# Two small DMAs on another queue, reordered scores, and roots on another engine, in a fused attention and expert kernel

## The chip, the cores and the metric

The kernel runs on one core of one Trainium2 chip. The core has five engines with instruction queues of their own: TensorE (matrix products and transposes, PE in the profile, its weight loads PEld), VectorE (DVE), ScalarE (ACT), GpSimd (POOL) and SyncE (SP, which here only issues DMAs). Each engine works through its queue in order; engines wait for each other through semaphores. ScalarE and POOL can issue DMAs too, each on a queue of its own. The metric is the device time of one execution in microseconds, lower is better.

## The reference

Sixty-four batches of 256 tokens with 256 features go through two layers. Each layer is a graph attention with a residual, then a feed-forward part with a residual; each of the four parts begins with a normalization of every row.

```python
def _layernorm(x, axis=-1, eps=1e-5):
    m = jnp.mean(x, axis=axis, keepdims=True)
    v = jnp.var(x, axis=axis, keepdims=True)
    return (x - m) / jnp.sqrt(v + eps)

# --- layer 0 (adj_ffn) ---
x = x + _L0_gnn_ref(_layernorm(x, axis=-1), adj, L0_gnn_W, L0_gnn_a)
x = x + _L0_ffn_ref(_layernorm(x, axis=-1), L0_ffn_weight, L0_ffn_bias)
# --- layer 1 (adj_ffn) ---
x = x + _L1_gnn_ref(_layernorm(x, axis=-1), adj, L1_gnn_W, L1_gnn_a)
x = x + _L1_ffn_ref(_layernorm(x, axis=-1), L1_ffn_router_w, ...)
```

The first attention has four heads of 64, leaky scores e_src[i] + e_dst[j] masked by the adjacency, a softmax over j and an ELU; the second has one head and a ReLU. The last part is a mixture of eight experts (256 to 256, GELU, 256 to 256), of which each token uses two, chosen by a router and weighted by a softmax over the two.

## The kernel before

**Batches.** One generator, `batch_layers`, holds the work of one batch: the first norm and projection (L569 to L575), the scores and the attention with four heads (L584 to L609), the linear layer (L611 to L628), the second attention (L629 to L653), the last norm (L655 to L662), then the row `xe` for the experts and the router's logits (L664 to L706). A batch is spread over several steps of an outer loop (L1194), and a new batch begins every third step (`TICKS = 3`), so several batches are in flight at different stages.

**Order.** The order of instructions on each engine is written out by hand. A generator yields a rank, and within a step the pieces of all active jobs are issued by rising rank (L1222 to L1229). A positive rank ends the job's part of this step; a negative one (`yield -36`) continues in the same step at rank 36. All queues follow this order, so an instruction with a higher rank stands behind the others of its step on its engine.

**The terms.** For the first attention the terms of a batch that lie along the columns are turned on VectorE (`ut`, L505), written to DRAM by a 4 KB DMA (L579) and read back spread over all 128 partitions by a second DMA of 512 KB (L514), which has to wait until the first has landed. Both are issued by SyncE, among the loads of later batches and, in the first 80 us, the loads and repacking of the eight experts' weights (`pack_expert`, L278). VectorE then computes the scores in two halves of four instructions (L530): the first at rank 10, the second at rank 70. Between them, at rank 40, come the reciprocals of the second attention of an earlier batch (L551), and ScalarE needs those for `rel` (L644).

**The norms.** For a norm, VectorE's batch statistics (L375, L376) or squares on ScalarE with accumulation (L402) give the variance; POOL computes (variance + eps)^-0.5 with two small instructions (L383 and L384, or L412 and L415). Two norms of different batches share one pair of these instructions, as their values are put in one tile: the first waits for the second, or for the end of the step (L1230 to L1233).

**Experts.** The rows of the first 61 batches are sent to DRAM regions, one for each expert, by indirect DMAs of POOL (L1011). They come back as pairs of 128 rows (`expert_pair`): loads on SyncE, a transpose on VectorE (L117), the first product (L903), two Gelus on ScalarE (L909), the second product (L918), the bias (L928), the row weight (L896). POOL then adds each pair's rows to the output by two indirect DMAs (L939). Adds of one pair wait until those of the pair before have landed, since they may meet in a row. Copies on ScalarE need no function table; Exp and Gelu lie in different tables, and a switch is an instruction of its own (ACT_TABLE_LOAD). The last three batches are computed for all experts without routing (`dense_expert`, L957). From step `DRAIN_AT` (three steps for each of B - 5 batches) pairs are started in every step; the stage after the last batch has begun is called the drain here.

**The transposes.** The linear layer's result x2 is transposed on TensorE in four pieces (L421) and copied by ScalarE (L427), at rank 36. The first product of a pair stands at rank 30, so it comes first. The projection of the second attention (L472, one step later) needs the copy.

Of the kernel before, what the change touches and what calls it, by code (L numbers as in the profile page):

```python
# [27 lines left out]
def kernel(  # L28
# [17 lines left out]
    nc = tc.nc  # L46
    B, N, D = x.shape
# [4 lines left out]
    NT = N // P  # L52
    EPS = 1e-5
# [6 lines left out]
    CHUNKS = (4,) * 12 + (2,) * 5 + (1,) * 3  # L60
# [9 lines left out]
    TICKS = 3  # L70
# [4 lines left out]
    small = ctx.enter_context(tc.tile_pool(name="small", bufs=4))  # L75
# [49 lines left out]
        return ap.rearrange("p (a k) -> p k a", k=KT)  # L125

    AHEAD, BLOCKS_AHEAD = 3, 2


    ident = const.tile([P, P], F32, tag="ident", name="ident")  # L130
# [228 lines left out]


    half_done = []

    def norm_stats(src):

        stats = small.tile([P, NT, 6], F32, tag="stats", name="stats")
        if half_done:
            mv, rstd = half_done[0]
            at = NT
        else:
            mv = small.tile([P, 2 * NT, 2], F32, tag="mv", name="mv", bufs=4)  # L370
            rstd = small.tile([P, 2 * NT], F32, tag="rstd", name="rstd", bufs=5)
            half_done.append((mv, rstd))
            at = 0
        for t in range(NT):
            nc.vector.bn_stats(stats[:, t, :], src[:, t, :])  # L375
            nc.vector.bn_aggr(mv[:, at + t, :], stats[:, t, :])  # L376
        if at:
            finish_norms(2 * NT)
        return mv[:, at : at + NT, :], rstd[:, at : at + NT]

    def finish_norms(n):
        mv, rstd = half_done.pop()
        nc.gpsimd.tensor_scalar_add(rstd[:, :n], mv[:, :n, 1], EPS)  # L383
        nc.gpsimd.tensor_tensor(rstd[:, :n], rstd[:, :n], mhalf[:, :n], ALU.pow)  # L384

    half_squared = []
# [3 lines left out]

    def norm_squares(src, sums):
        if half_squared:
            sq, rstd = half_squared[0]
            at = NT
        else:
            sq = small.tile([P, 2 * NT], F32, tag="sq", name="sq", bufs=4)
            rstd = small.tile([P, 2 * NT], F32, tag="rstd", name="rstd", bufs=5)
            half_squared.append((sq, rstd))
            at = 0
        for t in range(NT):  # L400
            off = work.tile([P, D], F32, tag="off", name="off", bufs=1)
            nc.scalar.activation(  # L402
                off, src[:, t, :], AF.Square, bias=sums[:, t : t + 1], scale=-float(D),
                accum_out=sq[:, at + t : at + t + 1],
            )
        if at:
            finish_squares(2 * NT)
        return rstd[:, at : at + NT]

    def finish_squares(n):  # L410
        sq, rstd = half_squared.pop()
        nc.gpsimd.tensor_scalar(  # L412
            rstd[:, :n], sq[:, :n], 1.0 / D**3, EPS, op0=ALU.mult, op1=ALU.add
        )
        nc.gpsimd.tensor_tensor(rstd[:, :n], rstd[:, :n], mhalf[:, :n], ALU.pow)  # L415
# [44 lines left out]
    for i in range(2):  # L460
        t = keep.tile([P, NT, D + 1], F32, tag=f"q1_{i}", name=f"q1_{i}")
# [39 lines left out]
    def send_terms(q, b):  # L501


        ut = small.tile([P, S], F32, tag="ut", name="ut", bufs=1)
        nc.vector.transpose(  # L505
            ut.rearrange("p (t h w) -> p t h w", t=NT, h=H), q[:, :, :, HD - 1 : HD + 3]
        )
        ud = tc.dram_tile([S, S], F32, name=f"terms_{b}")
        ud = ud.rearrange("c r -> (c r)").rearrange("(c p) -> c p", p=P)
        return ut, ud  # L510

    def spread_terms(ud, z):

        nc.sync.dma_start(  # L514
            out=z[:, NT - 1].rearrange("p t h i -> p (t h i)"),
            in_=rows_to_all(ud, S * S),
        )

    def scores(q, z, hs, spread):

        for h in hs:
            terms = z[:, NT - 1, :, h, :]
            if not spread:
                terms = bank("pd", [NT, P])
                for t in range(NT):
                    nc.tensor.transpose(
                        terms[:, t, :], q[:, t, h, HD + 1 : HD + 2].to_broadcast([P, P]), ident
                    )
            for j in range(NT):
                nc.vector.scalar_tensor_tensor(  # L530
                    z[:, j, :, h, :], terms, q[:, j, h, HD + 2 : HD + 3],
                    masks[0][:, j, :].rearrange("p (t i) -> p t i", t=NT),
                    op0=ALU.max, op1=ALU.mult,
                )
# [19 lines left out]
    def batch_layers(b, c0, xng, lg):  # L554

        def first_norm():
            x0 = xin.pop(b)
            if b + AHEAD < B:
                xin[b + AHEAD] = load_batch(b + AHEAD)
            return x0, norm_stats(x0)[1]  # L560

        if b:
            x0, rstd = first_norm()
# [6 lines left out]
        if not b:  # L570
            x0, rstd = first_norm()
# [4 lines left out]
        if b:  # L576
            ut, ud = send_terms(q, b)
            yield -31
            nc.sync.dma_start(  # L579
                out=ud.rearrange("c (g r) -> g c r", g=G),  # L580
                in_=ut[2 : P : S // (NT * H), :],
            )
            yield -52
        z = work.tile([P, NT, NT, H, P], F32, tag="z4", name="z4", bufs=2)  # L584
        if b:
            spread_terms(ud, z)
        yield 99
        yield 10
        scores(q, z, range(0, 2), b > 0)
        yield -70  # L590
        scores(q, z, range(2, 4), b > 0)
# [19 lines left out]
        _, rstd = norm_stats(x1)  # L611
# [24 lines left out]
        z = scores1(ex, me)  # L636
# [367 lines left out]
        active.append([rank, len(order), job])  # L1004
        order.append(job)

    order, order_steps = [], []

    def send(xe, at):

        d = nc.gpsimd.indirect_dma_start(  # L1011
            out=xs_d[: E * CAP * PAIR, :],
            out_offset=bass.IndirectOffsetOnAxis(ap=at, axis=0), in_=xe, in_offset=None,
        )
        tc.declare_no_dep(
            d.ins, query=SYNC, group="rows", reason="sent rows are all different, and none is in a full pair"
        )
        tc.add_to_no_dep_group("rows", d.ins)
        sent.append(d.ins.name)
        nc.gpsimd.nop()  # L1020
# [166 lines left out]
    step, more, credit = 2, True, 0.0  # L1187


    DRAIN_AT = TICKS * (B - 5)  # L1190
    SETUP_AT = 4
    dense_free = 0
    with tc.manual_schedule():
        while more or active or waiting or dense_jobs or scatters:  # L1194
            phase = step % TICKS
            if more and (phase == 0 or step == 2):
                nxt = next(batches, None)
                more = nxt is not None
                if more:
                    begin(nxt, 40 if phase == 0 else 25)  # L1200
            if step >= SETUP_AT and setup:
                begin(setup.pop(0)(), 90)
# [12 lines left out]
            if scatters:  # L1215
                def one():
                    scatter()
                    return
                    yield
                begin(one(), 97)  # L1220
            order_steps.append(step)
            queue = [(a[0], a[1], a) for a in active]  # L1222
            heapq.heapify(queue)
            while queue:
                *_, entry = heapq.heappop(queue)
                entry[0] = next(entry[2], None)
                if entry[0] is not None and entry[0] < 0:
                    entry[0] = -entry[0]
                    heapq.heappush(queue, (entry[0], entry[1], entry))  # L1229
            if half_done:  # L1230
                finish_norms(NT)
            if half_squared:
                finish_squares(NT)  # L1233
            active[:] = [a for a in active if a[0] is not None]
            step += 1

# [34 lines left out]
```

## Time and profile before

| | us |
|---|---|
| median of four runs | 1530.04 (1526.99 to 1533.24) |
| profiled execution, its own time | 1524.33 |
| its span, first to last instruction | 1522.6 |
| TensorE busy | 1431.5 (94%) |
| VectorE busy | 1249.9 (82%) |
| ScalarE busy | 1004.6 (66%) |
| POOL busy | 876.8 (58%) |

The times of the engines overlap, so a share says only how full an engine is on average; which engine sets the pace differs from stage to stage. In lines of the timeline the columns are start (us from the span's start), duration, engine, line and operation, out<-in, shapes, count, and in brackets how long the engine was idle before and which instruction or DMA ended that. A line of waits gives the total, the number and the longest. SPq is SyncE's queue.

### The profile page before, as it was taken

How to read it: one execution, taken by the hardware profiler on the slowest of the kernel's cores; microseconds unless marked ns; L12 is line 12 of the kernel's file. 1: busy time of each engine (PE TensorE's matmuls, PEld its weight loads, DVE VectorE, ACT ScalarE, POOL GpSimd, SP SyncE). 2: the span in 40 equal slices, each digit the busy share in tenths (PEclk: the TensorE clock that was granted, in tenths of full speed). 3: DMA queues.
4: the chain of work that ended last, by engine and by line, in shares of the span. 5: the costliest groups of instructions: out<-in, count | busy, mean ns of one | idle time of the engine just before them, and what ended most of it. 6: DMA issues, size and time to landing. Idle time of an engine off the chain costs nothing. (4 is left out here: it accounts for less than half of the span.)

```text
span 1522.6 us, 29896 instructions
## 1 busy us (share of the span) xinstructions
PE 1431.5 (94%) x8066; PEld 1266.1 (83%) x8066; DVE 1249.9 (82%) x4392; ACT 1004.6 (66%) x2379; POOL 876.8 (58%) x853
## 2 busy tenths in 40 slices
PE   6799998899999999999999999998999998779996
PEld 5688877789999998989998989997878787668885
DVE  7699899989998888888998889999887877645543
ACT  1366556577777777787777777776677778554331
POOL 2121445355867676766767575856756676544444
PEclk9899999999999999999999999999999999899998
DMA  5843354567887877777878787867787666787753
GB/s 148 232 125 97 104 139 121 137 170 164 185 180 174 175 172 179 175 169 172 185 173 179 159 193 161 197 142 165 174 182 172 135 146 143 172 168 163 148 100 52
DMA packets 372851, 240.84 MB, mean 158 GB/s; under 512 B 264772, under 2 KB 334924, under 8 KB 372684
## 3 DMA queue, kind: packets, MB, share of 16 engines
q1 hardware_dynamic: 322828, 171.60, 45.3%
q0 software_dynamic: 48864, 66.33, 23.7%
q8 instruction: 67, 1.10, 0.3%
q10 hardware_dynamic: 992, 0.99, 0.2%
q14 instruction: 100, 0.82, 0.2%
HBM read 150.46 MB, written 88.35 MB: 157 GB/s over the span
## 5 line engine op out<-in xcount | busy, mean ns | idle before, releaser
L939 POOL DMA_INDIRECT out_dram<-y,xt x258 | 412.9, 1600 | 186.6 <-issue 65.0
L544 PE MATMUL pv<-q,z 128*128 128x65 f32 (+1 forms) x2560 | 368.7, 300 | 0.4
L544 PEld LDWEIGHTS pv<-q,z 128*128 128x128 f32 x2560 | 335.9, 196 | 13.1 <-DVE z L530 1.1
L1011 POOL DMA_INDIRECT xs<-xng,pos x244 | 265.5, 1088 | 65.3 <-issue 61.2
L918 PE MATMUL py<-w2s,hT 128*128 (+1 forms) x1224 | 286.1, 385 | 7.8 <-ACT hT L909 6.8
L918 PEld LDWEIGHTS py<-w2s,hT 128*128 128x128 f32 x1224 | 232.0, 193 | 41.1 <-ACT hT L909 9.2
L903 PE MATMUL ph<-sT,we 128*128 128x256 f32 x1032 | 239.8, 382 | 7.2 <-DVE sT L117 4.3
L530 DVE SCALAR_TENSOR_TENSOR z<-z,q,mask 128x256 f32<-128x256 f32 x504 | 232.2, 482 | 14.8 <-DMA z<-terms 5.8
L903 PEld LDWEIGHTS ph<-sT,we 128*128 128x128 f32 x1032 | 196.3, 192 | 35.0 <-DVE sT L117 5.1
L427 ACT COPY xT<-pt 128x512 f32<-128x512 f32 x192 | 113.6, 592 | 109.3 <-PE pt L421 85.3
L896 ACT ACTIVATE y<-y,w 128x256 f32<-128x256 f32 x258 | 112.9, 499 | 107.2 <-DVE y L928 94.1
L383 POOL TENSOR_SCALAR rstd<-mv 128x4 f32<-128x4 f32 (+1 forms) x67 | 15.9, 237 | 261.6 <-DVE mv L376 200.1
L909 ACT ACTIVATE hT<-ph,we 128x256 f32<-128x256 f32 x306 | 123.7, 473 | 61.5 <-PE ph L903 41.3
L472 PE MATMUL pq<-wx,xT 128*128 128x259 f32 x512 | 130.4, 398 | 18.0 <-ACT xT L427 13.8
L402 ACT ACTIVATE off<-x,sums 128x256 f32<-128x256 f32 x256 | 129.4, 505 | 11.2 <-issue 2.7
L928 DVE TENSOR_TENSOR y<-py,b2s 128x512 f32<-128x512 f32 x129 | 85.8, 686 | 58.9 <-PE py L918 37.1
L437 PE MATMUL pq<-wx,xT 128*128 128x268 f32 x512 | 129.5, 397 | 2.8 <-DVE xT L117 2.2
L644 ACT ACTIVATE rel<-pv,rinv 128x256 f32<-128x256 f32 x128 | 53.6, 469 | 117.6 <-DVE rinv L551 91.5
L472 PEld LDWEIGHTS pq<-wx,xT 128*128 128x128 f32 x512 | 96.6, 195 | 40.6 <-ACT xT L427 20.4
L618 PE MATMUL pf<-wfT,xT 128*128 128x256 f32 x512 | 125.7, 390 | 0.0
L437 PEld LDWEIGHTS pq<-wx,xT 128*128 128x128 f32 x512 | 99.1, 194 | 22.5 <-DVE xT L117 1.4
L618 PEld LDWEIGHTS pf<-wfT,xT 128*128 128x128 f32 x512 | 96.0, 198 | 11.4 <-issue 0.3
(164 smaller groups left out, 2373.7 us busy)
## 6 DMA issues: line engine op xcount, KB each, us to landing
we<-wpack SPq DMA_DIRECT2D x145, 288.0 KB
xr<-xs SPq DMA_DIRECT2D x516, 64.0 KB
z<-terms SPq DMA_DIRECT2D x63, 512.0 KB
xblk<-in_x_dram SPq DMA_DIRECT2D x256, 64.0 KB
xin<-in_x_dram SPq DMA_DIRECT2D x64, 256.0 KB
out_dram<-base SPq DMA_DIRECT2D x61, 256.0 KB
out_dram<-y,xt POOLq DMA_INDIRECT x258
xs<-xng,pos POOLq DMA_INDIRECT x244
```

The costliest lines, as they stand in the source:

```text
L402: nc.scalar.activation(off, src[:, t, :], AF.Square, bias=sums[:, t : t + 1], scale=-float(D), accum_out=sq[:, at + t : at + t + 1],)
L427: nc.scalar.copy(dst, pt)
L437: nc.tensor.matmul(pq.rearrange("p h c -> p (h c)"), xT[:, k, t * P : (t + 1) * P], wx[:, k, :], start=(k == 0), stop=(k == KT - 1),)
L472: nc.tensor.matmul(pq, xT[:, k, t * P : (t + 1) * P], wx1[:, k, :], start=(k == 0), stop=(k == KT - 1),)
L530: nc.vector.scalar_tensor_tensor(z[:, j, :, h, :], terms, q[:, j, h, HD + 2 : HD + 3], masks[0][:, j, :].rearrange("p (t i) -> p t i", t=N ...
L544: nc.tensor.matmul(pv[:, h, :], z(j, h, t), q[:, j, h, : d + 1], start=(j == 0), stop=(j == NT - 1),)
L618: nc.tensor.matmul(pf[:, t, :], xT[:, k, t * P : (t + 1) * P], wfT[:, k, :], start=(k == 0), stop=(k == KT - 1),)
L903: nc.tensor.matmul(ph[:, f, :], we[:, k * D + f * P : k * D + (f + 1) * P], xT[:, k, :], start=(k == 0), stop=(k == KT - 1),)
L909: nc.scalar.activation(hT[:, f, :], ph[:, f, :], AF.Gelu, bias=we[:, C_B1 + f : C_B1 + f + 1])
L918: nc.tensor.matmul(py[:, t, :], hT[:, f, t * P : (t + 1) * P], w2s[:, e, f * D : (f + 1) * D].rearrange("p e c -> p (e c)"), start=(f == 0 ...
L939: d = nc.gpsimd.indirect_dma_start(out=out_rows, out_offset=bass.IndirectOffsetOnAxis(ap=xt[:, t, 0:1].bitcast(I32), axis=0), in_=y[:, t, ...
L1011: d = nc.gpsimd.indirect_dma_start(out=xs_d[: E * CAP * PAIR, :], out_offset=bass.IndirectOffsetOnAxis(ap=at, axis=0), in_=xe, in_offset=None,
```

## The change

- For batches 1 to 17 (`SETTLED` is 18) the two DMAs of the terms are issued by ScalarE instead of SyncE, in the same places of the order by rank.
- For batches below 11 (`PAIRED`) the first half of the scores moves from rank 10 to rank 42, behind the reciprocals of the second attention. Where these exist in the same step, batches 3 to 10, VectorE now has two reciprocals, then all eight score instructions.
- In steps from `DRAIN_AT` on the transposes of x2 move from rank 36 to 29. This concerns the last eight batches: on TensorE the four transposes stand ahead of L903, and on ScalarE their copy stands ahead of the table load and the two Gelus of that pair.
- In steps from 3 x (B + 2) on, which only the last two batches reach with these norms, VectorE computes the inverse roots: one instruction for variance plus eps, one for a first guess from the bits, and three rounds of three instructions. This happens four times (once for a norm from statistics, three times for squares), 11 instructions each, in place of POOL's two. For squares a new function `settle` issues them at rank 12 of the same step. Before those steps `settle` does nothing, and the ranks that follow are the old ones.

```diff
+    PAIRED = CHUNKS[0] + CHUNKS[1] + 3
+    SETTLED = CHUNKS[0] + CHUNKS[1] + CHUNKS[2] + CHUNKS[3] + 2
...
+    def at_end():
+        return order_steps[-1] >= TICKS * (B + 2)
+
+    def inverse_root(y, v):
+
+        n = v.shape[-1]
+        t = small.tile([P, 2 * NT], F32, tag="root", name="root", bufs=2)[:, :n]
+        nc.vector.tensor_scalar(
+            y.bitcast(I32), v.bitcast(I32), -0.5, float(0x5F3759DF), op0=ALU.mult, op1=ALU.add
+        )
+        for _ in range(3):
+            nc.vector.tensor_tensor(t, y, y, ALU.mult)
+            nc.vector.scalar_tensor_tensor(t, t, -0.5, v, op0=ALU.mult, op1=ALU.mult)
+            nc.vector.scalar_tensor_tensor(y, t, 1.5, y, op0=ALU.add, op1=ALU.mult)
+
     def finish_norms(n):
         mv, rstd = half_done.pop()
+        if at_end():
+            var = small.tile([P, 2 * NT], F32, tag="sq", name="var", bufs=4)[:, :n]
+            nc.vector.tensor_scalar(var, mv[:, :n, 1], EPS, None, op0=ALU.add)
+            inverse_root(rstd[:, :n], var)
+            return
         nc.gpsimd.tensor_scalar_add(rstd[:, :n], mv[:, :n, 1], EPS)
         nc.gpsimd.tensor_tensor(rstd[:, :n], rstd[:, :n], mhalf[:, :n], ALU.pow)
...
-        if at:
-            finish_squares(2 * NT)
+        if at and not at_end():
+            finish_squares()
         return rstd[:, at : at + NT]
 
-    def finish_squares(n):
-        sq, rstd = half_squared.pop()
+    def settle():
+        if half_squared and at_end():
+            finish_squares()
+
+    def finish_squares():
+        sq, rstd, n = half_squared.pop()
+        if at_end():
+            nc.vector.tensor_scalar(
+                sq[:, :n], sq[:, :n], 1.0 / D**3, EPS, op0=ALU.mult, op1=ALU.add
+            )
+            inverse_root(rstd[:, :n], sq[:, :n])
+            return
...
-    def spread_terms(ud, z):
+    def terms_queue(b):
 
-        nc.sync.dma_start(
+        return nc.scalar if b < SETTLED else nc.sync
+
+    def spread_terms(b, ud, z):
+
+        terms_queue(b).dma_start(
             out=z[:, NT - 1].rearrange("p t h i -> p (t h i)"),
             in_=rows_to_all(ud, S * S),
         )
...
             yield -31
-            nc.sync.dma_start(
+            terms_queue(b).dma_start(
                 out=ud.rearrange("c (g r) -> g c r", g=G),
                 in_=ut[2 : P : S // (NT * H), :],
             )
...
         yield 99
-        yield 10
+        yield 10 if b >= PAIRED else 42
         scores(q, z, range(0, 2), b > 0)
         yield -70
         scores(q, z, range(2, 4), b > 0)
...
         rstd = norm_squares(x2, sums)
-        yield -36
+        yield -12
+        settle()
+        yield -29 if order_steps[-1] >= DRAIN_AT else -36
         xT = transposed(x2)
...
         rstd = norm_squares(x2, sums)
+        yield -12
+        settle()
         yield 8
```

More of the change, by code (lines that the diff above doesn't have):

```diff
@@ L361 @@
     half_done = []
+    DRAIN_AT = TICKS * (B - 5)
+    order, order_steps = [], []
     def norm_stats(src):
@@ L392, in norm_squares @@
         if half_squared:
-            sq, rstd = half_squared[0]
-            at = NT
+            sq, rstd, at = half_squared.pop()
         else:
@@ L397, in norm_squares @@
             rstd = small.tile([P, 2 * NT], F32, tag="rstd", name="rstd", bufs=5)
-            half_squared.append((sq, rstd))
             at = 0
+        half_squared.append((sq, rstd, at + NT))
         for t in range(NT):
@@ L585, in batch_layers @@
         if b:
-            spread_terms(ud, z)
+            spread_terms(b, ud, z)
         yield 99
-        yield 10
+        yield 10 if b >= PAIRED else 42
         scores(q, z, range(0, 2), b > 0)
@@ L1005, in begin @@
         order.append(job)
-    order, order_steps = [], []
     def send(xe, at):
@@ L1187 @@
     step, more, credit = 2, True, 0.0
-    DRAIN_AT = TICKS * (B - 5)
     SETUP_AT = 4
@@ L1232 @@
             if half_squared:
-                finish_squares(NT)
+                finish_squares()
             active[:] = [a for a in active if a[0] is not None]
```

## The prediction

> **What bounds the kernel now.** I read the busy time by stages first, then the timeline of the stages that the change touches, then the waits, and last the scatters at the end.
>
> ```profile
> core 0: us, PE busy (x) PEld busy (x) DVE busy (x) ACT busy (x) POOL busy (x), PEclk, DMA share, GB/s
> 75.00:325.00 250.00, 234.25 (x1423) 205.60 (x1424) 230.33 (x813) 158.75 (x429) 94.62 (x125) 0.97 0.47 126
> 325.00:1025.00 700.00, 698.59 (x4141) 630.71 (x4139) 629.08 (x2161) 535.79 (x1265) 476.35 (x446) 1.00 0.78 174
> 1150.00:1300.00 150.00, 136.20 (x722) 118.57 (x721) 119.03 (x498) 118.03 (x246) 104.09 (x94) 0.95 0.70 149
> 1300.00:1358.00 58.00, 43.23 (x167) 34.87 (x166) 27.85 (x126) 30.71 (x65) 31.09 (x26) 0.85 0.80 175
> 1358.00:1500.00 142.00, 141.03 (x651) 123.49 (x652) 73.29 (x178) 55.80 (x127) 62.48 (x41) 1.00 0.67 129
> ```
>
> Before the experts start, VectorE sets the pace (230 of 250 us); in the middle TensorE does (699 of 700), and the change touches nothing there. From 1150 us no engine is full: batches and expert pairs wait for each other. The setup, before 75 us, has one large stall:
>
> ```profile
> 52.13 0.52 SPq L579 DMA_DIRECT2D terms<-ut  x1
> 55.09 0.34 SPq L514 DMA_DIRECT2D z<-terms  x1
> 60.28 1.92 DVE L530 SCALAR_TENSOR_TENSOR z<-z,q,mask 128x256 f32<-128x256 f32 x4 [4.65 <-DMA z<-terms]
> 62.31 0.84 ACT L644 ACTIVATE rel<-pv,rinv 128x256 f32<-128x256 f32 x2 [7.98 <-DVE rinv L551]
> 63.36 0.35 PE L491 MATMUL pd<-ident,ex 128*128 128x128 f32 x1 [4.25 <-ACT ex L479]
> ```
>
> The terms of batch 3 were ready at 49.34 (L505, 49.13 + 0.21), but SyncE sent them at 52.13, behind an expert's weight loads. So the scores waited 4.65 us, the reciprocals queued behind them held ScalarE, and ScalarE held TensorE.
>
> The end is this:
>
> ```profile
> 1496.11 0.91 ACT L896 ACTIVATE y<-y,w 128x256 f32<-128x256 f32 x2 [1.67 <-DVE y L928]
> 1506.08 1.54 POOL L939 DMA_INDIRECT out_dram<-y,xt  x1 [3.08 <-DMA out_dram<-y,xt]
> 1512.55 1.54 POOL L939 DMA_INDIRECT out_dram<-y,xt  x1 [3.08 <-DMA out_dram<-y,xt]
> ```
>
> The last pair's result is ready at 1497.02 and scattered from 1512.55: each pair waits until the pair before has landed. In pair order, results lie ready 10 to 19 us before their scatter from 1240 us on. The chain of waits follows TensorE (L918, L903, 5% each), but I take the scatters on POOL to be what ends last. TensorE time saved in the drain then counts only where POOL itself waits for a batch:
>
> ```profile
> 1197.54 0.23 POOL L383 TENSOR_SCALAR rstd<-mv 128x4 f32<-128x4 f32 x1 [6.02 <-DVE mv L376]
> 1237.73 0.20 POOL L412 TENSOR_SCALAR rstd<-sq 128x4 f32<-128x4 f32 x1 [1.36 <-ACT off L402]
> 1264.22 0.25 POOL L412 TENSOR_SCALAR rstd<-sq 128x4 f32<-128x4 f32 x1 [3.70 <-ACT off L402]
> 1266.81 2.02 PE L472 MATMUL pq<-wx,xT 128*128 128x259 f32 x8 [2.40 <-ACT xT L427]
> 1289.07 0.25 POOL L412 TENSOR_SCALAR rstd<-sq 128x4 f32<-128x4 f32 x1
> 1289.40 1.04 POOL L415 TENSOR_TENSOR rstd<-rstd,mhalf 128x4 f32<-128x4 f32 x1
> 1344.35 0.16 DVE L659 SCALAR_TENSOR_TENSOR by<-sums,rstd 128x2 f32<-128x2 f32 x1 [10.14 <-POOL rstd L415]
> ```
>
> **Early terms and scores.** Two DMAs of each of batches 1 to 17 leave SyncE for ScalarE; all else on SyncE moves up. On ScalarE each pair costs 0.55 us (L579) and 0.35 us (L514) of issue, and the second waits until the first has landed, 1.69 us after its start in a regular batch (97.51 to 99.20). Behind it stand the copy of a transposed tile and the exponential e. That wait lies under base (1.14 us, issued between; in batches 1 to 4 ScalarE was idle there). The cover is ScalarE's own waiting: between 75 and 325 us 57.8 us for reciprocals, 13.9 for hp and 10.9 for transposes, 82.6 in 16 batches or 5.2 us each. Cost taken: nothing; without cover 17 x 0.9 = 15 us. Moving the first half of the scores behind two reciprocals (batches 3 to 10) delays it by 0.23 us each and leaves VectorE's work the same; the layer-1 product was done 0.4 us before the scores began at 91.29 (L544 ended 90.88), so no wait is added. Cost nothing; if TensorE ran a microsecond later, 8 x 0.6 = 5 us.
>
> Gain: ScalarE is free from 45.83 to 52.11, so batch 3's terms go at 49.4 and the spread at 49.4 + 1.7 = 51.1 instead of 55.09. With the same landing (60.28 - 55.09 = 5.2) it lands at 56.3; VectorE arrives at 60.28 - 4.65 = 55.6. That leaves 0.7 of 4.65: 4.0 us gained. With its gap of 4.25 us gone (the reciprocals no longer wait for the spread) TensorE should keep its clock: after the gap the product L544 took 6.93 us instead of 3.68, and VectorE waited 2.84 for it and 1.74 for L618, 4.6 us. Together 8.6; I take 8. Lower bound 0 (the spread lands no sooner). Upper 14: plus 1.2 of batch 2's wait and 4.2 of VectorE's waits at L625 between 75 and 325 us, which follow a half clock behind another gap at L491 (1.46 us).
>
> **Transposes ahead of the expert product.** In eight batches four transposes (0.60 us) and their copy (0.59) pass an expert's L903 and its two Gelus with their table load (1.28). It removes TensorE's waits at L472 for that copy: 9.7 us in six places between 1130 and 1312, 2.2 to 2.4 each in four. The new wait is for x2 (L625): in six batches a product of 1.9 us lies between L618 and the transposes and covers it; in two nothing does, 1.24 us each by the row at 52.53. The pair's Gelu comes 0.6 us later, hidden by the 10 us and more that results lie ready; without that cover 8 x 0.6 = 5 us. Batch flow gains 9.7 - 2.5 = 7 us, and of the end as much as POOL's waits above allow: 6.02 + 1.36 + 3.70 = 11.1 at most. At 1197 the batches are some 2.2 us ahead (waits of 0.36, 2.21 and 0.35 gone, the two new ones paid, and 1.75 for a clock of 0.93 between 1150 and 1175); by 1264 four more waits are gone, more than the rest needs. 2.2 + 1.4 + 3.7 = 7.3; ScalarE, busy 24.46 of 25 us between 1250 and 1275, will take some back. Taken: 5, between 0 and 9.
>
> **Roots by VectorE.** Four pairs of POOL instructions (about 1.0 to 1.4 us each) become 11 small VectorE ones, 0.2 us apart by such rows (L764 to L767): 2.2 us each, 9 in all, in a stretch where VectorE is busy 28 of 58 us. Before a root VectorE now waits for ScalarE's squares, and the routing and results behind it wait too; that is less than the 10.14 and 6.40 us that it waited for POOL. For the end only POOL's queue counts: the root at 1289.07 stands between scatters and sends, 1.4 us; the other three lie under a landing. Taken 1.4; from -1 (VectorE's added work reaches the sends) to 3.
>
> **Sum.** 8 + 5 + 1.4 = 14.4 us off the profiled execution's 1524.33 (span 1522.6), which ran 5.7 us under the median. Off the median: 1530.0 - 14.4 = **1516**, own range 1508 to 1524.
>
> **Rivals.**
> 1. *Only the early part arrives*: 1530 - 8 - 1.4 = 1521 (1517 to 1525). For it: ScalarE nearly full at 1264, just where POOL waits. Against: its queue holds the copy back, not its work.
> 2. *The transfer sets the scores*: in 50 to 75 us the DMA engines are busy 0.82 at 233 GB/s, so an earlier issue need not land earlier; early gain 1: 1530 - 1 - 5 - 1.4 = 1523 (1518 to 1527). Against: SyncE's earlier loads stood ahead in the same queue. The Trainium skill ("DMA: Bandwidth & Descriptors", Issuing engines are not separate DMA queues) speaks for it: issue from several engines saves only issue time, since all share the same 16. The Trainium skill ("TensorE: Matmul & The Clock Gate", Part 1) halves the clock only after an idle window of about 3.4 us; by that rule even here the gap, cut to some 1.3 us, would spare the 4.6 and give 1519. The rows agree only in part: gaps of 2.2 us, too, were followed by a 0.93 clock.
> 3. *TensorE ends it*: then all its stalls count: 9.7 and 7.5 (clock 0.95 over 150 us), 1.53 + 2.80 + 3.45 before the late transposes, 25 in all with 8 before: 1497. For it 141 of 142 us busy; against it the 15 us for which the last results lie.
> 4. *Slower: ScalarE stands at its second DMA.* It pays 0.9 us plus what the terms' landing takes over 1.69; with 5.2 of cover it decides from a landing of 6.0 us. At 7 us: 17 x 1.0 = 17 lost, 6.4 won: 1541. Against it: SyncE's longest wait there was 2.6 us (median 0.6).
>
> **How the numbers follow.** Forecast 0.50, rivals 0.20, 0.14, 0.09, 0.07. 0.5% is 7.6 us, about what a measurement here tells from no change: faster is under 1522.4. Of the forecast 0.46, of rival 1 0.12, of rival 2 0.06, all of 3: 0.73. Slower is rival 4, 0.07; the rest 0.20. The range, 1502 to 1529, leaves out rival 4, most of rival 3 and the tails.
>
> **What would show it.** Right: the spread of batch 3 issued 4 us sooner after its terms, VectorE waiting under 1 us there, no half clock before 75 us; L472's waits gone between 1130 and 1312; VectorE's waits of 10 and 6 us gone; scatters still back to back, with the last result lying ready over 10 us. Wrong: a ScalarE that waits for DMAs in the first 300 us, new waits of the transposes for x2 above 2 us each, or a last scatter that follows its result at once.

## The result and the profile after

| | before | changed |
|---|---|---|
| median, us | 1527.65 (68 runs) | 1524.33 (42 runs) |
| ratio to before | | 0.997 (0.9956 to 0.9984) |
| profiled execution, its own time | 1524.33 | 1525.73 |
| its span | 1522.6 | 1524.0 |

The change gives 4.6 us (0.003 x 1527.65; interval 2.4 to 6.7), where 14.4 were forecast; the two medians differ by 3.3. The two profiled executions lie on the wrong sides of their medians, before 3.3 us under it and the changed one 1.4 over it, so their spans are not compared. What can be compared is how far an instruction of the same count (the n-th score, the n-th scatter) has moved from one profile to the other, and where that offset changes. In this table a minus is earlier in the changed kernel:

| n-th instruction, at (us in before) | offset, us |
|---|---|
| score at 78 | -4.1 |
| score at 196 | -5.5 |
| score at 332 | -7.5 |
| score at 1015 | -6.1 |
| result (L896, now L937) at 1119 | -1.0 |
| result at 1267 | -1.2 |
| last result, 1497 | -11.9 |
| scatter (L939, now L980) at 1102 | -5.3 |
| scatter at 1285 | -0.8 |
| last scatter, 1514 | +1.4 |

So 7 us are won before 332 us, mostly kept for 700 us, and mostly lost between 1075 and 1119 us (a result at 1075 still lies at -6.1); the results win 11 us again after 1267 us, and the scatters make nothing of that.

First the busy times by stages of the changed kernel, in the columns of before (engines' busy us and number of instructions, TensorE's granted clock, DMA share, GB/s):

```profile
core 0: us, PE busy (x) PEld busy (x) DVE busy (x) ACT busy (x) POOL busy (x), PEclk, DMA share, GB/s
75.00:325.00 250.00, 233.11 (x1442) 204.89 (x1440) 232.46 (x824) 164.81 (x435) 98.79 (x127) 0.99 0.47 134
325.00:1025.00 700.00, 697.80 (x4140) 629.78 (x4140) 627.87 (x2159) 531.84 (x1257) 473.41 (x448) 1.00 0.79 174
1150.00:1300.00 150.00, 136.80 (x725) 117.31 (x724) 123.32 (x527) 121.59 (x252) 101.52 (x90) 0.98 0.70 148
1300.00:1358.00 58.00, 44.88 (x206) 37.91 (x207) 35.63 (x162) 31.07 (x70) 27.73 (x22) 0.94 0.83 184
1358.00:1500.00 142.00, 138.26 (x636) 120.04 (x634) 71.27 (x164) 52.58 (x119) 62.53 (x40) 1.00 0.66 125
```

Before 325 us the clock is 0.99 instead of 0.97; from 1150 us it is higher too (0.98 and 0.94 for 0.95 and 0.85), and still the last scatter came no sooner. Next the timeline of the setup, at batch 3:

```profile
52.17 0.52 ACTq L616 DMA_DIRECT2D terms<-ut  x1
...
54.64 0.39 ACTq L551 DMA_DIRECT2D z<-terms  x1
...
59.47 0.23 DVE L588 RECIPROCAL rinv<-pv 128x1 f32<-128x1 f32 x2
59.61 3.73 DVE L567 SCALAR_TENSOR_TENSOR z<-z,q,mask 128x256 f32<-128x256 f32 x8
59.66 0.84 ACT L683 ACTIVATE rel<-pv,rinv 128x256 f32<-128x256 f32 x2 [1.52 <-DVE rinv L588]
...
63.09 3.68 PE L581 MATMUL pv<-q,z 128*128 128x65 f32 x32
```

The terms are sent by ScalarE (ACTq) 0.03 us after they were turned (51.93 + 0.21), but the spread leaves at 54.64, only 0.45 us sooner than before. The scores no longer wait; two reciprocals come before them, `rel` waited 1.52 instead of 7.98 us, and the product takes 3.68 us, the full-speed time, where before it took 6.93 after TensorE's gap of 4.25. ScalarE's waits in the first 325 us (total, number, longest) show the price:

```profile
engine line waited for: us in total, times, longest us
...
ACT e L640 <- DMA terms<-ut: 10.4, 1, 10.4
...
ACT xT L460 <- DMA terms<-ut: 5.3, 6, 1.9
```

At batch 2 ScalarE stood at its second DMA: the terms left at 36.98, the spread at 41.58, 4.6 us instead of the 1.69 of a regular batch, and the exponential behind it came 3.9 us later than before (42.06 for 38.18), 1.0 of it since its operand hp was later. That is the mechanism of the slower rival, in one batch; the six waits of the copy average 0.9 us.

The end, last result and last scatters of GpSimd:

```profile
1484.23 0.91 ACT L937 ACTIVATE y<-y,w 128x256 f32<-128x256 f32 x2 [1.67 <-DVE y L969]
...
1507.57 1.54 POOL L980 DMA_INDIRECT out_dram<-y,xt  x1 [3.00 <-DMA out_dram<-y,xt]
...
1513.96 1.54 POOL L980 DMA_INDIRECT out_dram<-y,xt  x1 [3.00 <-DMA out_dram<-y,xt]
```

The last result is ready at 1485.14 and its scatter starts 28.8 us later, back to back behind the landing of the pair before. Before, it lay 15.5 us.

The drain is where the gain went. Two stretches of the changed kernel's timeline, in brackets the idle time and what ended it:

```profile
1097.16 0.47 DVE L662 SCALAR_TENSOR_TENSOR x<-pf,rstd,x1b 128x256 f32<-128x256 f32 x1
...
1097.70 1.12 PE L454 MATMUL pt<-ident,x 128*128 128x128 f32 x4 [4.47 <-DVE x L689]
...
1098.61 5.65 PE L944 MATMUL ph<-sT,we 128*128 128x256 f32 x16
```

```profile
1221.14 1.84 POOL L980 DMA_INDIRECT out_dram<-y,xt  x1 [0.30 <-issue]
...
1223.29 1.57 POOL L980 DMA_INDIRECT out_dram<-y,xt  x1 [0.30 <-issue]
...
1225.25 0.73 POOL L408 TENSOR_TENSOR rstd<-rstd,mhalf 128x2 f32<-128x2 f32 x1
...
1226.01 0.48 DVE L662 SCALAR_TENSOR_TENSOR x<-pf,rstd,x1b 128x256 f32<-128x256 f32 x1 [3.81 <-POOL rstd L408]
...
1226.56 0.84 PE L454 MATMUL pt<-ident,x 128*128 128x128 f32 x4 [2.90 <-DVE x L662]
```

The same place in the kernel before:

```profile
1098.51 1.89 PE L618 MATMUL pf<-wfT,xT 128*128 128x256 f32 x8
...
1100.24 3.62 PE L903 MATMUL ph<-sT,we 128*128 128x256 f32 x16
...
1102.43 0.47 DVE L625 SCALAR_TENSOR_TENSOR x<-pf,rstd,x1b 128x256 f32<-128x256 f32 x1
...
1108.25 2.02 PE L472 MATMUL pq<-wx,xT 128*128 128x259 f32 x8 [1.37 <-ACT hT L909]
```

In the first stretch, TensorE stands 4.47 us at the moved transposes (L454) until VectorE has made x2 (L662); the expert's first product behind them then takes 5.65 us instead of 3.62 (L903 at 1100.24 in before): half clock for a part of it. 4.47 - 1.37 (the wait at 1108.25 of before, which is gone) + 2.03 = 5.1 us, about what the results lose from -6.1 to -1.0. The Trainium skill ("TensorE: Matmul & The Clock Gate", Part 1) lets the clock halve after an idle window of about 3.4 us. This gap agrees; the product L472 at 1159.34 of before, 3.62 us after a gap of 2.21 where others take 2.02, does not. Of the twelve gaps over 1 us at these transposes, in the four kernels below that have them moved, the five of up to 3.10 us were followed by an expert's product at full speed and the seven of 3.73 us and more by a slower one. The second stretch shows what x2 waits for: VectorE idles 3.81 us for the batch's root (L408) on GpSimd, and that root stands in GpSimd's queue behind the two scatters at 1221.14 and 1223.29. TensorE now waits for the queue of scatters. In the kernel before, the expert's product stood ahead of the transposes and covered this.

### The profile page after: what moved, and what is told of

Same layout as the page of the kernel before. It is cut to its first block, busy times and chain, and to the rows that moved or that the text cites. A ratio compares the mean times of both kernels' runs of the same rounds, so it can differ in the third digit from the quotient of the medians.

```text
span 1524.0 us, 29964 instructions
## 1 busy us (share of the span) xinstructions
PE 1423.0 (93%) x8066; PEld 1257.3 (83%) x8066; DVE 1255.8 (82%) x4436; ACT 1007.5 (66%) x2379; POOL 870.8 (57%) x845
## 3 DMA queue, kind: packets, MB, share of 16 engines
q0 software_dynamic: 48864, 66.33, 23.6%
## 5 line engine op out<-in xcount | busy, mean ns | idle before, releaser
L980 POOL DMA_INDIRECT out_dram<-y,xt x258 | 414.1, 1605 | 196.6 <-issue 66.5
L581 PE MATMUL pv<-q,z 128*128 128x65 f32 (+1 forms) x2560 | 365.1, 298 | 0.3
L581 PEld LDWEIGHTS pv<-q,z 128*128 128x128 f32 x2560 | 331.7, 194 | 12.9 <-DVE z L567 0.8
L1050 POOL DMA_INDIRECT xs<-xng,pos x244 | 260.8, 1069 | 65.5 <-issue 60.8
L959 PE MATMUL py<-w2s,hT 128*128 (+1 forms) x1224 | 280.6, 380 | 6.2 <-ACT hT L950 6.2
L959 PEld LDWEIGHTS py<-w2s,hT 128*128 128x128 f32 x1224 | 228.3, 190 | 38.1 <-ACT hT L950 9.0
L944 PE MATMUL ph<-sT,we 128*128 128x256 f32 x1032 | 245.1, 388 | 14.7 <-DMA we<-wpack 7.5
L937 ACT ACTIVATE y<-y,w 128x256 f32<-128x256 f32 x258 | 113.1, 499 | 113.9 <-DVE y L969 101.6
```

The costliest lines, as they stand in the source:

```text
L581: nc.tensor.matmul(pv[:, h, :], z(j, h, t), q[:, j, h, : d + 1], start=(j == 0), stop=(j == NT - 1),)
L937: nc.scalar.activation(y[:, t, :], y[:, t, :], AF.Copy, scale=w[:, t : t + 1])
L944: nc.tensor.matmul(ph[:, f, :], we[:, k * D + f * P : k * D + (f + 1) * P], xT[:, k, :], start=(k == 0), stop=(k == KT - 1),)
L959: nc.tensor.matmul(py[:, t, :], hT[:, f, t * P : (t + 1) * P], w2s[:, e, f * D : (f + 1) * D].rearrange("p e c -> p (e c)"), start=(f == 0 ...
L980: d = nc.gpsimd.indirect_dma_start(out=out_rows, out_offset=bass.IndirectOffsetOnAxis(ap=xt[:, t, 0:1].bitcast(I32), axis=0), in_=y[:, t, ...
L1050: d = nc.gpsimd.indirect_dma_start(out=xs_d[: E * CAP * PAIR, :], out_offset=bass.IndirectOffsetOnAxis(ap=at, axis=0), in_=xe, in_offset=None,
```

## The experiments

Each was timed against before on the chip it ran on (three chips in all), so rows are compared by their ratios. The offsets are those of the table above, taken in each kernel's own profile against the profile of before. Since single executions differ by several us from their first 80 us on, what counts in the drain is the change of the offset from one column to the next. The offsets of a row are those of one execution; those executions of c_only (1533.30 us) and queue_only (1521.98) were the longest of their kernels, 8.6 and 10.0 us over their medians.

| kernel | early part | moved transposes | late roots | last score of batch 12 | scatter at 1058 | scatter at 1285 | last result | last scatter | ratio (interval) |
|---|---|---|---|---|---|---|---|---|---|
| changed | yes | yes | yes | -5.5 | -6.1 | -0.8 | -11.9 | +1.4 | 0.9970 (0.9956 to 0.9984) |
| after_again | yes | yes | yes | -8.9 | -9.4 | -2.7 | -12.6 | +4.4 | 0.9971 (0.9945 to 0.9998) |
| no_c | yes | yes | | -5.2 | -3.4 | -1.4 | +0.4 | +0.1 | 0.9971 (0.9948 to 0.9994) |
| b_only | | yes | | +3.8 | +0.9 | +1.7 | +0.7 | +1.3 | 1.0011 (0.9985 to 1.0038) |
| c_only | | | yes | +4.1 | +3.6 | +2.9 | -3.1 | +9.0 | 0.9996 (0.9971 to 1.0022) |
| no_b | yes | | yes | -8.4 | -6.2 | -5.8 | -19.3 | -4.5 | 0.9954 (0.9927 to 0.9980) |
| a_only | yes | | | -9.5 | -10.5 | -10.9 | -11.4 | -10.8 | 0.9934 (0.9910 to 0.9959) |
| queue_only | queue | | | -3.6 | -6.7 | -6.6 | -6.5 | -2.3 | 0.9934 (0.9909 to 0.9960) |
| scores_only | order | | | -1.7 | -4.4 | -5.3 | -5.2 | -5.4 | 0.9987 (0.9960 to 1.0015) |
| a_copy_first | yes | copy only | | -6.4 | -4.3 | -11.4 | -10.7 | -12.3 | 0.9902 (0.9870 to 0.9933) |
| f_c | yes | copy only | yes | -7.2 | -8.4 | -14.9 | -23.6 | -12.3 | 0.9912 (0.9880 to 0.9944) |

**The parts by themselves.** The edits undo parts of the change:

```diff
 (a_only: both of these; b_only and c_only: one of them, without the early part; no_b: the first; no_c: the second)
-        yield -29 if order_steps[-1] >= DRAIN_AT else -36
+        yield -36
...
     def at_end():
-        return order_steps[-1] >= TICKS * (B + 2)
+        return False
```

The early part alone:

> Before with the early part alone (terms by ScalarE for batches 1 to 17, scores behind the reciprocals for batches 3 to 10). Theory 1 (the early part's 7 us, seen in the profile of the changed kernel as events 6.5 us earlier from 325 to 1025 us, reach the end; the moved transposes took back what they gave and a little more): 6 to 7 us faster than before, ratio 0.9955 to 0.996, so 2 to 3 us faster than the whole change; in the profile TensorE's waits for the copy at L505 are back and every scatter after 1060 us comes 5 to 7 us sooner than before. Theory 2 (the scatters on GpSimd set the end and the early gain is lost in them): within 2 us of before, ratio 0.999 to 1.001, and the whole change's gain must come from the drain. Theory 3 (the profiled execution misleads: the early part gives 3 to 4 us as measured, the drain nothing): ratio 0.997 to 0.998.

Measured: 0.9934, 10.1 us faster (6.3 to 13.7). Theory 1 stands, theory 2 falls: the scatters from 1058 us on are 6 to 12 us earlier, most of them 10 to 11 and the last 10.8, though the last result still lies ready for 16.1 us. Here the offset that the batches have when the drain begins goes through the whole chain of scatters.

The moved transposes alone:

> Before with the moved transposes alone (rank 29 from DRAIN_AT on). Theory 1: the six waits at the projection of 9.7 us go and waits of 4.5, 2.9 and three of 0.5 us for x2 ahead of the transposes come, with a half clock behind the long one; the end moves by 0 to 4 us to the slower side, ratio 1.000 to 1.003. Theory 2 and the prediction: 3 to 5 us faster, ratio 0.9967 to 0.998. Theory 3: within 1 us, 0.9995 to 1.0005.

Measured: 1.0011 (0.9985 to 1.0038), 1.7 us slower by the middle value; the interval excludes the 5 us of the prediction. The profile has the new waits at 1103, 1231 and 1285 us, 4.32, 3.73 and 6.76 us. The timeline around the last of them shows the whole path:

```profile
1280.18 1.61 POOL L980 DMA_INDIRECT out_dram<-y,xt  x1 [1.03 <-DMA out_dram<-y,xt]
...
1282.10 1.58 POOL L980 DMA_INDIRECT out_dram<-y,xt  x1 [0.30 <-issue]
...
1284.07 0.73 POOL L408 TENSOR_TENSOR rstd<-rstd,mhalf 128x2 f32<-128x2 f32 x1
...
1284.84 0.48 DVE L662 SCALAR_TENSOR_TENSOR x<-pf,rstd,x1b 128x256 f32<-128x256 f32 x1 [7.51 <-POOL rstd L408]
...
1285.39 1.12 PE L454 MATMUL pt<-ident,x 128*128 128x128 f32 x4 [6.76 <-DVE x L662]
...
1286.29 3.37 PE L944 MATMUL ph<-sT,we 128*128 128x256 f32 x8
```

The scatter at 1280.18 waited for the landing of the pair before, the second followed, then the root (L408) at 1284.07; VectorE idled 7.51 us for it, TensorE 6.76, and the product after that took 3.37 us for eight matmuls that take 1.97 at full clock.

The late roots alone:

> Before with VectorE's roots in the last two batches alone. All theories: the scatters of the end bound it, so 0 to 1.5 us faster, ratio 0.999 to 1.000; VectorE's two long waits for GpSimd's roots in the last two batches go and the last results are ready 8 to 12 us sooner, yet the last scatter starts as before. If instead the last results set the end, 8 us faster, ratio 0.995.

Measured: 0.9996. In the profile the last result comes 3.1 us sooner, 6.7 us gained on the offset at 1058, and the last scatter 9.0 us later, in the longest of the twelve executions. Results do not set the end here.

Early part and roots, without the moved transposes:

> The changed kernel with the transposes back at rank 36: early part and roots. Theory 1: 7 to 9 us faster than before, ratio 0.994 to 0.9955, thus 3 to 4 us faster than the whole change; the waits of 4.5 and 2.9 us ahead of the transposes in the drain are gone. Theory 2 (the drain's transposes bring the gain): within 2 us of before. Theory 3: as the whole change, 0.997.

Measured: 0.9954, 7.0 us faster (3.1 to 11.1), as theory 1 has it. The last results are 19.3 us earlier and lie ready for 30.3 us.

The whole change again, and without the roots:

> The changed kernel once more, on the chip of the three runs beside it. All theories: ratio to before 0.996 to 0.998; the moved transposes wait for x2 near 1097 us (4 to 5 us), 1226 us (2 to 3 us) and 1277 us (1.5 us) again, or the waits are an accident of one execution and lie elsewhere with half the sum.

> The changed kernel with GpSimd's roots in the last two batches: early part and moved transposes. If the roots on VectorE cost 2 to 3 us (the stretch from the 97th scatter to the last was 228.4, 229.2 and 233.2 us long in the three profiles with them, 226.4 to 231.3 and mostly 227.0 in those without): 2 to 3 us faster than the whole change, ratio 0.994 to 0.996, and that stretch 226 to 228 us. If they gain the predicted 1.4 us: 1 to 2 us slower than the whole change, ratio 0.997 to 0.999. The moved transposes alone then account for a loss of 2 to 5 us against the early part alone (0.9934).

Measured: 0.9971 for both. So the roots neither cost nor gave anything here; the early part with the moved transposes (no_c) is 5.6 us slower than the early part alone (0.0037 x 1527; by the two intervals some 0.5 to 10.8). The waits for x2 come back in each kernel with the moved transposes, near 1095, 1225 and 1280 us, with sizes that vary: from 1050 to 1300 us they sum to 9.5, 11.0, 15.1 and 15.1 us (changed, after_again, no_c, b_only), where before has one of 1.5 us. From the scatter at 1058 to that at 1285 these four lose 5.3, 6.7, 2.0 and 0.8 us, 3.7 in the mean; the five without moved transposes or copy change by -0.9 to +0.4.

**Queue and order of the early part.**

```diff
 (queue_only: scores as in before)
-        yield 10 if b >= PAIRED else 42
+        yield 10
...
 (scores_only: queue as in before)
-        return nc.scalar if b < SETTLED else nc.sync
+        return nc.sync
```

> Before with ScalarE's issue of the terms for batches 1 to 17 alone; the scores stay at rank 10. Theory Q (the earlier issue is what pays, as predicted): 7 to 10 us faster than before, ratio 0.9935 to 0.9955, the wait at batch 3's scores under 1.5 us and TensorE's gap of 4.25 us ahead of L524 gone. Theory O (the order pays: the reciprocals no longer stand behind a late transfer): 0 to 3 us faster, ratio 0.998 to 1.000; batch 3's spread is issued within 1 us of 55.1, as in the changed kernel (54.64), the scores still wait for it by 2 us or more and TensorE's gap stays near 3 us.

> Before with the first half of the scores at rank 42 for batches below 11 alone; SyncE issues all terms. Theory Q: within 2 us of before, ratio 0.9985 to 1.0015, since the scores wait for the same transfer. Theory O: 6 to 9 us faster, ratio 0.994 to 0.996: at batch 3 the reciprocals run at 57 to 59 us instead of 62.1, TensorE's gap ahead of L524 is under 1 us and no half clock follows it before 76 us, and the last score of batch 14 comes 6 to 9 us sooner than without it.

Measured: 0.9934 for the queue, 0.9987 (0.9960 to 1.0015) for the order. Theory Q stands in the times, but the spread did not leave 4 us sooner, as it had it. The timeline of the queue alone at batch 3:

```profile
54.24 0.39 ACTq L551 DMA_DIRECT2D z<-terms  x1
...
58.45 1.92 DVE L567 SCALAR_TENSOR_TENSOR z<-z,q,mask 128x256 f32<-128x256 f32 x4
...
60.29 0.23 DVE L588 RECIPROCAL rinv<-pv 128x1 f32<-128x1 f32 x2
...
62.21 3.68 PE L581 MATMUL pv<-q,z 128*128 128x65 f32 x32
```

The spread leaves at 54.24, again hardly sooner, and the scores follow at 58.45 without a wait: the transfer took 4.2 us or less, where in before it took 5.2. With the order alone the stall only moves on:

```profile
55.12 0.34 SPq L551 DMA_DIRECT2D z<-terms  x1
...
59.34 3.75 DVE L567 SCALAR_TENSOR_TENSOR z<-z,q,mask 128x256 f32<-128x256 f32 x8 [0.16 <-DMA z<-terms]
...
77.44 3.75 DVE L567 SCALAR_TENSOR_TENSOR z<-z,q,mask 128x256 f32<-128x256 f32 x8 [5.09 <-DMA z<-terms]
...
78.07 6.21 PE L581 MATMUL pv<-q,z 128*128 128x65 f32 x27 [2.03 <-DVE z L567]
```

Batch 3 waits 0.16 us, but at batch 4, whose terms SyncE sends 3.7 us after they were turned (68.94 for 65.21), VectorE waits 5.09 us and TensorE 2.03, and the product behind it runs at half clock (6.21 us for 27 of 32 matmuls). The Trainium skill ("DMA: Bandwidth & Descriptors", Issuing engines are not separate DMA queues) has it that issuing from another engine saves only issue time. Here the issue that came out from behind the weight loads was worth 10 us. In the profile of queue_only the score at 78 us lies 5.6 us sooner, behind the stall and the half clock that before has there; where the rest comes from was not traced.

**The transposes' copy without the transposes.** In the drain the two Gelus of a pair go behind the copy on ScalarE; TensorE's order stays that of before.

```diff
-        hT = hidden(xT, we)
+        ph = first_product(xT, we)
+        if order_steps[-1] >= DRAIN_AT:
+            yield -38
+        hT = gelus(ph, we)
         yield -65
...
```

> The early part alone, and in the drain the two Gelus of a pair move behind the copy of the transposes on ScalarE (rank 38 in place of 30), while the order on TensorE stays that of before: what the moved transposes were to bring, without their wait for x2. Theory 1 (the wait for x2 took back the gain): TensorE's waits of 2.2 to 2.4 us ahead of L505 in the drain fall below 1 us and no wait over 1 us stands ahead of the transposes; the batches in the drain run 3 to 7 us ahead of the early part alone by 1260 us, the end 1 to 5 us, ratio to before 0.990 to 0.993. Rival (the drain's TensorE time reaches nothing, or the later Gelu costs as much): ratio 0.993 to 0.995, batches by 1260 us less than 2 us ahead.

Measured: 0.9902 (0.9870 to 0.9933), some 15 us faster than before and 4.9 faster than the early part alone by the middle values (their intervals overlap). TensorE's waits from 1050 to 1300 us, first of the early part alone, then with the copy first:

```profile
PE pq L505 <- ACT xT L460: 15.3, 9, 2.3
```

```profile
PE pq L505 <- ACT xT L460: 3.3, 2, 3.0
...
PE pt L454 <- DVE x L662: 0.8, 1, 0.8
```

One of 3.0 us stayed, against the expectation; the rest is gone, and no wait for x2 above 0.8 us took its place. With the roots in both kernels (f_c, below, against no_b) the same step is worth 0.0042 or 6.4 us, so the gain was seen twice, though neither pair alone is clear of noise. From 1058 to 1285 us the scatters gain 7.1 us, the batches with them, and the end 8.0.

**The end.** With the late roots on top:

> The run with the copy ahead of the Gelus (order of TensorE as before), and VectorE's roots in the last two batches with it: the whole change with its transposes replaced. If the roots cost as the stretch from the 97th scatter to the last hints (231 us mean in four profiles with them, 228 in eight without): ratio to before 0.9915 to 0.9935 and that stretch 229 us or longer. If the roots cost nothing or gain 1.4 us: ratio 0.989 to 0.991 and the stretch 225 to 228 us.

Measured: 0.9912 (0.9880 to 0.9944), the stretch from the scatter of the 97th pair (at 1285 us in before) to the last 229.6 us long. The ratio lies between the two expectations, the stretch is that of roots that cost. The end of this kernel's profile:

```profile
1472.48 0.91 ACT L940 ACTIVATE y<-y,w 128x256 f32<-128x256 f32 x2 [1.62 <-DVE y L978]
...
1493.81 1.54 POOL L989 DMA_INDIRECT out_dram<-y,xt  x1 [3.08 <-DMA out_dram<-y,xt]
...
1500.21 1.54 POOL L989 DMA_INDIRECT out_dram<-y,xt  x1 [3.02 <-DMA out_dram<-y,xt]
```

The last result is ready at 1473.39, 23.6 us before that of before and 12.9 before that of the copy first alone, and its scatter starts 26.8 us later, at the same place as without the roots (1500.04). This shows the chain of scatters as what ends last, most plainly of all runs.

Then the scatters themselves were moved ahead, in the early part alone and in the version with the copy first; in the second run a result finished in the same step is also taken:

```diff
-                begin(one(), 97)
+                begin(one(), 20 if step >= DRAIN_AT else 97)
...
```

> The early part alone, and in steps from DRAIN_AT on the scatter of the oldest result moves from rank 97 to rank 20, ahead of that step's root from statistics and sends: one pair fewer stands behind the last root on GpSimd (24 in place of 25). Theory S (the scatter chain sets the end, results lie ready 16 us): 4 to 6.5 us (one period of 6.5) faster than the early part alone, ratio to before 0.989 to 0.991, last lag about 10 us. Rival R (GpSimd's scatters now hold up the roots, and the batches with them): 0 to 6 us slower than the early part alone, ratio 0.9935 to 0.998, the root of the statistics at 1134 and 1187 us later by 3 us and more and with it the results.

> As the run before, but the scatter at rank 20 takes also a result that was finished in the same step: two pairs fewer stand behind the last root (23 in place of 25). Theory S: 9 to 13 us faster than the early part alone as long as results still lie ready, ratio to before 0.985 to 0.988, last lag 3 to 6 us. Rival R: GpSimd waits for results ahead of the roots; as slow as before or slower, ratio 0.996 to 1.003.

> The run with the copy ahead of the Gelus, and the scatter of the oldest result at rank 20 in the drain. Theory S (one pair fewer behind the last root on GpSimd): 3 to 6 us faster than without, ratio 0.986 to 0.9885. Rival R (the scatters hold up roots that are now due sooner): 0 to 3 us slower than without, ratio 0.990 to 0.992.

Measured: 0.9923 (0.9895 to 0.9950), 0.9928 (0.9896 to 0.9961) and 0.9902 (0.9868 to 0.9936). In the profiles the scatters move from 1058 to the end by -4.3 and -9.0 us against -0.3 of the early part alone, so one or two periods as theory S has it (the second profile is an execution 5 us under its median); the times show no more than 2 us of that, and with the copy first nothing (-6.3 against -8.0). Whether the rest is lost because the scatters hold up the roots (in f_scat20 the results lose 2.1 us from 1075 to 1119) was not isolated.

**More roots on VectorE.** The early part alone, with `at_end` true from `DRAIN_AT` on:

```diff
-        return False
+        return order_steps[-1] >= DRAIN_AT
```

> The early part alone, and VectorE computes all roots from DRAIN_AT on (some 18 pairs of GpSimd instructions become 11 small ones on VectorE each, 2.2 us). Theory S (GpSimd's queue sets the end, and its waits of 10.6, 6.0 and 3.2 us for statistics stand between scatters): the scatters from 1150 to 1300 us come 10 us and more sooner, the last 6 to 12 us sooner than with the early part alone, ratio 0.985 to 0.990. Rival V (VectorE, which had 31 us to spare of 150 between 1150 and 1300, becomes the bound with 40 us more, and the sends wait for the batches all the same): 0 to 15 us slower than the early part alone, ratio 0.9935 to 1.003, with the last results later.

Measured: 1.0023 (1.0002 to 1.0044), 13.6 us slower than the early part alone by the ratios (0.0089 x 1525). Rival V is right. The windows from 1150 to 1300 us, early part alone, then with all roots of the drain on VectorE:

```profile
core 0: us, PE busy (x) PEld busy (x) DVE busy (x) ACT busy (x) POOL busy (x), PEclk, DMA share, GB/s
...
1150.00:1300.00 150.00, 134.19 (x710) 116.86 (x709) 114.92 (x501) 118.17 (x247) 101.83 (x91) 0.96 0.69 147
```

```profile
core 0: us, PE busy (x) PEld busy (x) DVE busy (x) ACT busy (x) POOL busy (x), PEclk, DMA share, GB/s
...
1150.00:1300.00 150.00, 132.06 (x683) 114.59 (x682) 132.78 (x585) 110.05 (x230) 79.47 (x64) 0.93 0.68 142
```

VectorE goes from 114.92 to 132.78 us of 150, GpSimd from 101.83 to 79.47, and the scatters at 1285 are 5.4 us later than before instead of 10.9 earlier: by these rows the sends between them wait for the batches, and the batches for VectorE.

## Why the prediction was wrong

**The early part was right in sum.** Forecast 8 us between 0 and 14; measured 10.1 alone. TensorE's gap, the slow product and VectorE's waits behind it went as described. Not right was the way: the terms did not go at 49.4 with the spread at 51.1 but at 52.17 and 54.64, since batch 3 was itself 2.8 us late. Of that, 0.8 us were there before the terms of batch 2 were turned (36.74 for 35.92); the rest came in the step to batch 3, which took 14.8 to 15.4 us in the twelve profiles with ScalarE's issue and 13.2 to 14.1 in the four without. So the issue by ScalarE costs some 1 to 2 us there, which the forecast of 49.4 left out, and that the sum of the part came out is in part luck. The scores' move, priced at nothing, is worth nothing that can be told from zero (0.9987).

**The moved transposes are the step that failed.** "The new wait is for x2 (L625): in six batches a product of 1.9 us lies between L618 and the transposes and covers it; in two nothing does, 1.24 us each" - 2.5 us in all; 9.5 to 15.1 were measured (1.5 in before), plus half clocks behind them. Nor did the covering product suffice: at 1226 one of 1.89 us (L959) lies between, and TensorE still waits 2.90 us. The 1.24 came from a row of the setup, in which VectorE stood ready and GpSimd had no scatters. In the drain x2 stands behind other work on VectorE (4.47 us at 1097) and needs a root that stands in GpSimd's queue behind two scatters and what they wait for (2.90 to 6.76 us). The prediction asked what the old wait had cost and not what the old order had covered: the expert's product, 2 to 3.6 us long, hid just this. Instead of +5 the part gave -1.7 us alone (b_only, not clear of zero) and -5.6 on top of the early part (no_c against a_only). The other half of the step holds: freed waits at the projection do reach the end in the profile of a_copy_first, by 7 to 8 us; its times give 4.9, within the noise of two such runs. The way is the one forecast: GpSimd's waits for the batches' statistics fall from 18.9 us in a_only to 13.0 there between 1058 and 1290 us. Two signs that the prediction named for being wrong were there: a ScalarE that waits for a DMA at batch 2, and waits for x2 above 2 us.

**The end was read rightly.** Scatters stay back to back, the last result lies 28.8 us ahead of its scatter, and VectorE's waits of 10.14 and 6.40 us are gone without moving the end. The rival in which TensorE ends it is out.

**The late roots did not give their 1.4 us.** Four pairs of kernels with and without them differ by +0.0020, 0, -0.0004 and +0.0010 of the ratio, 1.0 us slower in the mean, with intervals of 4 us or more each. The stretch from the scatter of the 97th pair to the last was 229.2, 234.1, 228.4, 233.2 and 229.6 us with them (mean 230.9) and 225.9 to 231.3 without (mean 227.8 over ten). A cause is only argued: results come sooner, loads with them, and the waits for GpSimd become waits for transfers, as in the changed kernel at 1335 us:

```profile
1335.26 0.71 DVE L117 STREAM_TRANSPOSE sT<-xr 128x512 f32<-128x512 f32 x1 [6.98 <-DMA xr<-xs]
...
1337.40 3.75 PE L944 MATMUL ph<-sT,we 128*128 128x256 f32 x8 [7.48 <-DMA we<-wpack]
```

Between a loss of 3 us and nothing this stays open; a gain is not seen.

Of the rivals the first, in which only the early part arrives (1521), came nearest in its account. It allowed the drain to give nothing, but not to take. By the number the second (1523) lies nearer, by luck: its early gain of 1 us and its drain of 5 are both wrong. (Its lower figure of 1519 is 1518 by its own terms.)

## What to carry to other kernels

Before an instruction is moved ahead, follow what its operand needs through every queue, to the engine that issues the slowest thing there: a root that is two short instructions is as late as the DMA landing it stands behind. If the aim is to free a copy, move what delays the copy rather than what feeds it; here two Gelus put back on ScalarE removed the waits for the copy without the new waits that four transposes put forward on TensorE brought. And where a chain of landings ends the program, earlier results are worth nothing there, but an offset gained before the chain fills can go through it whole, as in the early part alone (10.5 us at 1058, 10.8 at the end).

## What was not expected of the hardware

Single executions of the changed kernel spread over 17 us (1516.09 to 1533.15), and with the clock granted to TensorE: those at 0.971 to 0.973 took 1527.8 us in the mean, those at 0.977 to 0.981 took 1520.7. Which of the two brings about the other is not shown. The clock already differs where the work is the same: a product of 32 matmuls (L581 at 29.3 us) took 7.28 us in a_only and 5.40 in a_copy_first, which have the same instructions there. The two profiles of the changed kernel differ by 3 us at batch 12 (-5.5 and -8.9). A part of a change that is worth less than 5 us is better read as a change of the offset inside its own stage. A pair of scatters takes 6.4 us where no more pairs are loaded (the mean of the last eight periods in before; 6.4 to 6.6 in the others) and 7.3 us in the mean while pairs are still loaded (1316 to 1441 us in before), without a change of its own instructions.
